# The token's mean as a ninth router column, its variance from ScalarE's squares, and the output bias added in DRAM

## The chip, the cores and the metric

The kernel runs on one core of one Trainium2 chip. The metric is the device time of one execution in microseconds (us), taken as the median of repeated executions. The profile is one further execution, recorded by the hardware profiler; it gives every instruction with its engine, start and duration. The engines are TensorE (PE in the profile; PEld is its weight load), VectorE (DVE, `V` in the code), ScalarE (ACT, `S`), GpSimd (POOL, `G`) and the sync engine (SP, `nc.sync`), which only issues DMAs. L1105 means line 1105 of the kernel.

## What is computed

A hybrid of deformable convolution, attention over the images of the batch and a mixture of experts, on `x` of 4 images, 256 channels, 64 x 64 positions, all in float32:

```python
x = x + conv(group_norm(x), w_off, b_off, w_conv)   # deformable 3x3, 256 -> 256
t = tokens(x)                                       # (4, 4096, 256)
mn = layernorm(t) * gamma + beta
q, k, v = mn @ Wq, mn @ Wk, mn @ Wv                 # 8 heads of 32
g = sigmoid(mn @ Wg + bg)
att = softmax(einsum('slhc,tlhc->sth', q, k) * scale, axis=1)   # s, t: the 4 images
t = t + (einsum('sth,tlhc->slhc', att, v) * g) @ Wo + bo
u = layernorm(t)                                    # no gain, no bias
logits = u @ router_w.T                             # 8 experts, the best 2 of each token
t = t + u + sum over the 2 experts of weight * (gelu(u @ w1 + b1) @ w2 + b2)
x = images(t)
```

A token is one position of one image: there are 16,384, and each has two rows (one for each of its experts).

## The kernel before

It runs in stages, one after the other, with the stages' edges overlapping a little.

**Preparation**, to some 99 us of the span: group norm's statistics, and tables of the images for the gathers.

**A, the deformable convolution** (99 to 2131 us). For each 128 positions and each of 9 taps, POOL gathers four neighbours of 256 channels by an indirect DMA (L577), ACT and DVE weigh and sum them (L593, L601), PE transposes the result (L615), ACT copies it to SBUF (L621) and PE multiplies it by the tap's weights (L640). The weight has 264 columns (`CR = C + NE`, L33): 256 channels, and 8 more that hold the product of the weight with the router's matrix. So a token comes out with its part of the router's logits beside it. The router's columns of a weight are made by `routed` (L133); the image's own part is a small matmul at L634. The sum with the image goes to DRAM as `t1[b][j]`, rows of 264 floats, for image b and block j of 512 positions.

**B, layernorm, q and k** (2131 to 2443 us). For each of 8 blocks and 4 images the loop at L801 loads `t1` (L805), normalizes it (`layernorm`, L176, whose variance goes to POOL's power by `rstd_of`, L162), transposes it into `mn`, projects q and k, and sums their products for the attention's logits (L825).

**D, attention output and routing** (2443 to 2884 us), one call of `block(j)` (L1116) for each of the 8 blocks, with all four images. Its steps, by name:

- `value` projects v of one image and half of the channels (PE); for image 0 ACT writes the first term of the mix. `mixed` adds a further image's term (DVE, 4 instructions of 128x512, L942).
- `gate` is a projection with a sigmoid (PE, ACT L947); `gated` multiplies by it (DVE).
- `output` multiplies by `wo_sb`, again 264 columns wide (L974). `residual` loads `t1` and adds the output bias `bo_sb`, also 264 wide (SP L958, DVE L959). `added` sums the two: the tokens in L988, their router logits in L990; in the first four blocks the tokens go to DRAM too (L994).
- `stats` takes the token's mean and variance by `bn_stats` and `bn_aggr` (DVE, L1001 and L1003, 4 of each an image) and has POOL raise the variance to the power -1/2 (L173). `shift` is minus mean times that (DVE, L1014), and `normed` writes the normalized rows into the tile `u` (ACT, L1021 for the column with the token's number, L1026 for the 256 values).
- `pick` finds the two experts of each token from the logits of all four images (DVE, L1039 to L1057), `count` sums by matmul how many tokens go to each (PE, L1070), and `placed` gives every row its slot (DVE, to L1096).
- `scatter(most)` issues up to that many of the 32 row scatters of a block: an indirect DMA of POOL (L1105) that writes 128 rows of `u` to their slots in `xs_rows`.

The routing of block j is finished inside block j+1: image 3's `shift` and `normed`, then `pick`, `count`, `placed` and all its scatters stand among the steps of the next block. The order of the instructions of PE, DVE and ACT is the one in which `block` writes them. POOL's and SP's is the scheduler's, except that `in_turn` (L153) keeps every power behind the scatters issued before it, and every scatter behind the last power. So a `stats` written behind `scatter(4)` has its power behind those four.

**The experts** (2884 to 3507 us): 142 tiles of 256 rows, each fetched from `xs_rows`, multiplied by its expert's two weights and scattered to `ys_rows`. The last block's routing is done among the first tiles, by a schedule `at(n, ...)` of steps between tile n and the next (L1454 to L1475). SP's and POOL's order is written out here as well (L1477). **The tail**, to 3577 us, adds the results up and stores them.

Of the kernel before, what the change touches and what calls it, by code (L numbers as in the profile page):

```python
# [9 lines left out]
F32 = mybir.dt.float32  # L10
# [22 lines left out]
CR = C + NE  # L33
# [37 lines left out]
def conv_attn_moe_kernel(  # L71
# [32 lines left out]
    nhalf = const.tile([P, 4], F32, name="nhalf")  # L104
# [27 lines left out]

    def routed(rows, rw, ps_turned, ps_out, pool, name):  # L133


        pr = ps_out.tile([P, len(rows), NE], F32, name=f"{name}_pr", tag="om")
        for n, w in enumerate(rows):
            tp = ps_turned.tile([P, C], F32, name=f"{name}_tp{n}", tag="tp")
            for ch in range(NCH):
                T.transpose(tp[:, ch * P : (ch + 1) * P], w[:, ch * P : (ch + 1) * P], ident)  # L140
            wT = pool.tile([P, C], F32, name=f"{name}_wT{n}", tag="sT")
            S.copy(wT, tp)
            for ch in range(NCH):
                T.matmul(
                    pr[:, n, :], wT[:, ch * P : (ch + 1) * P], rw[:, ch, :],
                    start=(ch == 0), stop=(ch == NCH - 1),
                )
        for n, w in enumerate(rows):
            V.tensor_copy(w[:, C:], pr[:, n, :])

    issued = []

    def in_turn(ins, others):  # L153

        for other in others:
            tc.add_manual_dep(
                ins.ins, other.ins.name,
                mybir.DependencyInfo(mybir.DependencyClass.NoSync, mybir.DependencyReason.DATA),
                reason="order of issue",
            )  # L160

    def rstd_of(pool, var, n, name, twice=False, into=None):  # L162


        ve = pool.tile([P, n], F32, name=f"{name}_ve", tag=f"ve{n}")
        if twice:
            V.tensor_scalar(ve, var, 1.0 + EPS, EPS * EPS, ALU.mult, ALU.add)  # L167
        else:
            V.tensor_scalar(ve, var, EPS, None, ALU.add)
        r = into  # L170
        if into is None:
            r = pool.tile([P, n], F32, name=f"{name}_rstd", tag=f"rstd{n}")
        issued.append(G.tensor_tensor(r, ve, nhalf[:, :n], ALU.pow))  # L173
        return r
# [24 lines left out]
    with ExitStack() as actx:  # L199
# [51 lines left out]
        rwc_sb = load_weight(aw, router_w, "rwc_sb")  # L251
# [507 lines left out]
    rw_sb = load_weight(dw, router_w, "rw_sb")  # L759
# [12 lines left out]
    with ExitStack() as bctx:  # L772
# [9 lines left out]
        with ExitStack() as ectx:  # L782
            et = ectx.enter_context(tc.tile_pool(name="e_t", bufs=1))
            ps_e = ectx.enter_context(tc.tile_pool(name="ps_e", bufs=1, space=PSUM))
            routed([wo_sb[:, ch, :] for ch in range(NCH)], rw_sb, ps_tp, ps_e, et, "wo")

            alike = et.tile([P, NCH, P], F32, name="alike")
            V.tensor_copy(alike, bo_c.unsqueeze(2).to_broadcast([P, NCH, P]))
            pb = ps_e.tile([P, 2, NE], F32, name="pb", tag="om")
            for n in range(2):  # L790
                for ch in range(NCH):
                    T.matmul(
                        pb[:, n, :], alike[:, ch, :] if n == 0 else ones, rw_sb[:, ch, :],
                        start=(ch == 0), stop=(ch == NCH - 1),
                    )
            V.tensor_copy(bo_sb[:, C:], pb[:, 0, :])
            V.tensor_copy(rsum, pb[:, 1, :])
        head_sum = block_diagonal(bw, "head_sum", DHEAD, 1.0)
        parts = bw.tile([P, NCH, B * B, NBLK], F32, name="parts")

        for j in range(NBLK):  # L801
            qs, ks = [], []
            for b in range(B):
                rows = bt.tile([P, NT, CR], F32, name=f"bt{b}_{j}", tag="t")
                nc.sync.dma_start(rows, t1[b][j])  # L805
                t = rows[:, :, :C]
                layernorm(bs, t, t, f"l1_{b}_{j}", twice=True)
                mn = channel_major(b, j)
# [21 lines left out]


# [84 lines left out]
    with ExitStack() as bctx:  # L916
# [36 lines left out]
        def residual(j, b):  # L953
            for i in range(0, NT, 2):
                t = ts[j, b, i] = bt.tile(
                    [P, 2, CR], F32, name=f"dt{b}_{j}_{i}", tag="t", bufs=4
                )
                nc.sync.dma_start(t, t1[b][j][:, i : i + 2])  # L958
                V.tensor_tensor(t, t, bo_sb.unsqueeze(1).to_broadcast([P, 2, CR]), ALU.add)  # L959
# [19 lines left out]
        def added(j, b):  # L979
            r = token_major(b, j)  # L980
            if b == 0:
                ss[j] = bs.tile([P, NG, NE], F32, name=f"s{j}", tag="s")
# [13 lines left out]
        def stats(j, b):  # L996
            x_ = token_major(b, j)
            st = bs.tile([P, NT, V.BN_STATS_DIM], F32, name=f"l3st{b}_{j}", tag="ln_st")
            mv = bs.tile([P, NT, V.BN_AGGR_DIM], F32, name=f"l3mv{b}_{j}", tag="ln_mv")
            for i in range(NT):  # L1000
                V.bn_stats(st[:, i, :], x_[:, i, :])  # L1001
            for i in range(NT):
                V.bn_aggr(mv[:, i, :], st[:, i, :])  # L1003
            rstd_of(
                bs, mv[:, :, 1], NT, f"l3_{b}_{j}", into=lns[j][0][:, b * NT : (b + 1) * NT]
            )
            in_turn(issued[-1], scattered)
            scattered.clear()
            lns[j, b] = mv

        def shift(j, b):
            r, nb = (x[:, b * NT : (b + 1) * NT] for x in lns[j])
            mv = lns.pop((j, b))
            V.scalar_tensor_tensor(nb, mv[:, :, 0], -1.0, r, ALU.mult, ALU.mult)  # L1014

        def normed(j, b):
            x_ = token_major(b, j)
            r, nb = lns[j]
# [4 lines left out]
            )  # L1023
            for i in range(NT):
# [8 lines left out]
        def pick(j):  # L1033


            r, nb = lns.pop(j)
            lg = ss.pop(j)
# [78 lines left out]
        def block(j):  # L1116
# [6 lines left out]
            value(j, 1, 1)  # L1123
            residual(j, 0)
            if last:
                shift(j - 1, 3)
                normed(j - 1, 3)
# [4 lines left out]
            mixed(j, 1, 0)  # L1132
            if last:
                count(j - 1)
            value(j, 2, 1)
            mixed(j, 1, 1)
            if last:
                placed(j - 1)
            scatter(14)
            value(j, 3, 0)  # L1140
            mixed(j, 2, 0)
            residual(j, 1)
            value(j, 3, 1)
            mixed(j, 2, 1)
# [11 lines left out]
            stats(j, 0)  # L1156
# [4 lines left out]
            shift(j, 0)  # L1161
            normed(j, 0)
            stats(j, 1)
            scatter(4)
            output(j, 2)
            residual(j, 2)
            gated(j, 3)
            output(j, 3)
            shift(j, 1)
            normed(j, 1)  # L1170
            added(j, 2)
            stats(j, 2)
            scatter(5)
            residual(j, 3)
            shift(j, 2)
            normed(j, 2)
            added(j, 3)
            stats(j, 3)
# [279 lines left out]
    def at(n, fn):  # L1458
        between.setdefault(n, []).append(fn)

    at(0, lambda: (shift(last, 3), normed(last, 3)))
    at(2, lambda: pick(last))
    at(3, lambda: count(last))
    at(4, lambda: placed(last))
    for n in range(6):
        at(6 + n, lambda: next(planning, None))
# [10 lines left out]
    with tc.manual_schedule(engines={nc.sync.engine, nc.gpsimd.engine}):  # L1477
        total = len(tiles)
# [76 lines left out]
```

## Time and profile before

| what | us |
|---|---|
| median of 14 runs | 3573.38 |
| lowest and highest of them | 3560.31, 3600.81 |
| the profiled execution | 3579.29 |
| its span, first to last instruction | 3577.5 |

| busy in the span | us | share | instructions |
|---|---|---|---|
| PE | 3052.5 | 85% | 13658 |
| DVE | 2600.9 | 73% | 6747 |
| POOL | 1973.3 | 55% | 1801 |
| ACT | 1719.8 | 48% | 3913 |

The groups that the change touches:

| instructions | count | busy us | mean ns |
|---|---|---|---|
| PE L640, 128x264 | 4608 | 1323.1 | 412 |
| PE L974, 128x264 | 512 | 118.0 | 386 |
| POOL L1105, row scatters | 256 | 261.4 | 1021 |
| DVE L942, mixes | 192 | 129.7 | 741 |
| POOL L173 in B, powers 128x4 | 32 | 34.4 | 1076 |

A busy share is an average over stages with different limits. It says which engine has how much to do, not what the end waits for. For that one needs the stage by itself (windows of time), and in it the order of the instructions of an engine with the idle time before each and what ended it.

### The profile page before, as it was taken

The numbers are of one execution on the slowest core, as the hardware profiler recorded it, in microseconds if no ns is written. First come the engines' busy times: TensorE is split into PE (matmuls) and PEld (weight loads), VectorE is DVE, ScalarE is ACT, GpSimd is POOL, SyncE is SP. The second block draws the span as 40 slices with busy tenths as digits, with TensorE's granted clock in tenths as the row PEclk, the third lists the DMA queues.
The fourth block names the chain that finished last, engine by engine and source line by source line (L and its number), as shares of the span: only waits on it lengthen the run. The fifth ranks groups of instructions, "written<-read, shape, count | busy, mean of one in ns | idle before, by whom it ended". The sixth has DMA issues, their size and how long they took to land. (4 is left out here: it accounts for less than half of the span.)

```text
span 3577.5 us, 49706 instructions
## 1 busy us (share of the span) xinstructions
PE 3052.5 (85%) x13658; PEld 2232.1 (62%) x13658; DVE 2600.9 (73%) x6747; ACT 1719.8 (48%) x3913; POOL 1973.3 (55%) x1801
## 2 busy tenths in 40 slices
PE   6799997889987899978778779897888888999995
PEld 4567766667766576756656654443444467888883
DVE  3777786867776777876767668887888864557777
ACT  2456654556554555644434434443333344556562
POOL 1665666666677665676776651110666656554441
PEclk7899998999998999988989989999999989999995
DMA  7889998899988899988778861112544344537778
GB/s 233 320 315 331 351 340 332 305 355 353 356 330 338 299 349 330 371 304 295 281 293 315 304 231 61 61 49 85 174 160 143 108 127 130 161 124 246 240 245 305
DMA packets 322442, 898.89 MB, mean 251 GB/s; under 512 B 43218, under 2 KB 89949, under 8 KB 320120
## 3 DMA queue, kind: packets, MB, share of 16 engines
q0 software_dynamic: 191808, 671.74, 51.7%
q1 hardware_dynamic: 130360, 223.98, 19.4%
q8 instruction: 113, 1.85, 0.2%
q14 instruction: 161, 1.32, 0.1%
HBM read 744.43 MB, written 154.79 MB: 251 GB/s over the span
## 5 line engine op out<-in xcount | busy, mean ns | idle before, releaser
L601 DVE SCALAR_TENSOR_TENSOR s<-g,wts,s 128x256 f32<-128x256 f32 x3456 | 1431.7, 478 | 522.5 <-ACT s L593 354.0
L577 POOL DMA_INDIRECT g<-table,idx x1152 | 1339.0, 1162 | 710.1 <-DVE s L601 426.9
L640 PE MATMUL acc<-wconv_sb,sT 128*128 128x264 f32 x4608 | 1323.1, 412 | 271.6 <-ACT sT L621 144.2
L640 PEld LDWEIGHTS acc<-wconv_sb,sT 128*128 128x128 f32 x4608 | 828.0, 200 | 412.7 <-ACT sT L621 170.7
L621 ACT COPY sT<-tps 128x256 f32<-128x256 f32 x1152 | 425.9, 370 | 756.2 <-PE tps L615 499.0
L593 ACT ACTIVATE s<-g,wts 128x256 f32<-128x256 f32 x1152 | 588.9, 511 | 213.5 <-DMA g<-table,idx 191.6
L615 PE MATMUL tps<-ident,s 128*128 128x128 f32 x2304 | 461.0, 283 | 38.6 <-DVE s L601 35.0
L615 PEld LDWEIGHTS tps<-ident,s 128*128 128x128 f32 x2304 | 326.2, 148 | 263.3 <-issue 174.1
L1379 POOL DMA_INDIRECT ys_rows<-y,to x284 | 283.5, 998 | 292.3 <-DVE y L1376 225.1
L1105 POOL DMA_INDIRECT xs_rows<-u,slots x256 | 261.4, 1021 | 128.4 <-issue 113.5
L1350 PE MATMUL ph<-xT,w 128*128 128x256 f32 x1136 | 280.0, 390 | 24.8 <-DVE second L1336 10.7
L1368 PE MATMUL py<-w,hT 128*128 128x256 f32 x1136 | 270.8, 382 | 0.0
L1373 DVE TENSOR_TENSOR y<-py,w 128x512 f32<-128x512 f32 x142 | 98.1, 691 | 204.3 <-ACT w L1312 71.1
L1354 ACT ACTIVATE hT<-ph,w 128x256 f32<-128x256 f32 x284 | 133.6, 474 | 233.4 <-PE ph L1350 177.0
L1350 PEld LDWEIGHTS ph<-xT,w 128*128 128x128 f32 x1136 | 209.8, 195 | 52.9 <-ACT hT L1354 11.6
L1368 PEld LDWEIGHTS py<-w,hT 128*128 128x128 f32 x1136 | 218.2, 192 | 30.5
L173 POOL TENSOR_TENSOR l_rstd<-l_ve,nhalf 128x4 f32<-128x4 f32 x32 | 34.4, 1076 | 252.5 <-DVE l_ve L167 252.5
L825 DVE SCALAR_TENSOR_TENSOR junk<-q,k 128x512 f32<-128x512 f32 x256 | 160.9, 681 | 9.9 <-ACT k L818 9.9
L396 PE MATMUL po<-xs,woff_sb 128*96 128x512 f32 x324 | 167.1, 601 | 0.0
L947 ACT ACTIVATE gate<-pg,bg_c 128x512 f32<-128x512 f32 x64 | 43.9, 686 | 248.0 <-PE pg L748 184.6
L942 DVE SCALAR_TENSOR_TENSOR mix<-pv,att,mix 128x512 f32<-128x512 f32 x192 | 129.7, 741 | 3.1 <-PE pv L748 3.1
L974 PE MATMUL po<-wo_sb,mix 128*128 128x264 f32 x512 | 118.0, 386 | 0.0
(245 smaller groups left out, 3363.5 us busy)
## 6 DMA issues: line engine op xcount, KB each, us to landing
xt<-xs_rows SPq DMA_DIRECT2D x142, 260.0 KB
table<-zt SPq DMA_DIRECT2D x128, 256.0 KB
early_state<-ys_rows SPq DMA_DIRECT2D x128, 256.0 KB
g<-table,idx POOLq DMA_INDIRECT x1152
t<-o SPq DMA_DIRECT2D x32, 528.0 KB
bt<-t SPq DMA_DIRECT2D x32, 528.0 KB
dt<-t SPq DMA_DIRECT2D x64, 264.0 KB
xraw<-in_x SPq DMA_DIRECT2D x16, 1024.0 KB
```

Of the source, the lines that this page charges most:

```text
L396: T.matmul(t["po"], woff_sb[:, ch, ki].rearrange("p kj o -> p (kj o)"), t["xs"][:, ch, ki : ki + RB], start=(n == 0), stop=(n == NCH * 3 - 1),
L577: g = G.indirect_dma_start(out=gs[n % NGB], out_offset=None, in_=tables[b], in_offset=bass.IndirectOffsetOnAxis(ap=params[b][0][:, r, k : ...
L593: first = S.activation(ss[n], gs[n % NGB][:, :C], AF.Copy, scale=params[b][1][:, 0, r, k : k + 1])
L601: last_corner[n] = V.scalar_tensor_tensor(ss[n], gs[n % NGB][:, c * C : (c + 1) * C], params[b][1][:, c, r, k : k + 1], ss[n], ALU.mult, A ...
L615: T.transpose(tps[n][:, ch * P : (ch + 1) * P], s[:, ch * P : (ch + 1) * P], ident)
L621: S.copy(sTs[n], tps.pop(n))
L640: T.matmul(accs[n // K2][:, :CR], sT[:, ch * P : (ch + 1) * P], wconv_sb[:, ch, k, :], start=False, stop=(k == K2 - 1 and ch == NCH - 1),)
L825: V.scalar_tensor_tensor(junk, qs[s_][:, ch, :], 1.0, ks[t_][:, ch, :], ALU.mult, ALU.mult, accum_out=parts[:, ch, s_ * B + t_, j : j + 1],)
L1105: s = G.indirect_dma_start(out=rows_, out_offset=bass.IndirectOffsetOnAxis(ap=slots[:, k, n : n + 1], axis=0), in_=u[:, n % NT, :], in_off ...
L1350: T.matmul(ph, w1_sb[:, ch, f * P : (f + 1) * P], xT[:, ch, :], start=(ch == 0), stop=(ch == NCH - 1),)
L1368: T.matmul(py[:, i, :], hT[:, f, i * P : (i + 1) * P], w2_sb[:, f, :], start=(f == 0), stop=(f == NCH - 1),)
L1379: s = G.indirect_dma_start(out=ys_rows[g], out_offset=bass.IndirectOffsetOnAxis(ap=to[:, i : i + 1], axis=0), in_=y[:, i, :], in_offset=No ...
```

## The change

**A ninth router column.** `NX = NE + 1` and `CR = C + NX` = 265. `load_router` fills the new column of the router's matrix with -1/256, so that a product with it is minus the mean of the 256 channels. Through `routed` the column goes into the convolution's weight, `wo_sb` and `bo_sb`; `t1` has rows of 265 floats; `ss[j]` holds eight logits and minus the mean of each token.

**The variance by ACT.** `stats` is gone, with its `bn_stats`, `bn_aggr` and power for each image. `squares` has ACT square each token's values with minus the mean as bias and sum them as it goes; the squares themselves are written to `u`, which `normed` overwrites later. `rstd(j, half)` takes the variances of two images at once: one DVE instruction and one power of 128x8. `shift` covers two images too.

**The output bias.** `residual` no longer adds `bo_sb`. In B, `with_bias` has POOL issue a DMA for each block and image that adds `bo_sb` to `t1` in DRAM, behind the layernorm of the next one. B's load takes 256 of a row's 265 floats.

**The order.** The power of images 2 and 3 moves to the next block, ahead of `mixed(j, 1, 0)`, and `shift` ahead of `mixed(j, 1, 1)`; `normed` of these images stands between later values. `mixed(j, 2, 0)` and `mixed(j, 2, 1)` stand ahead of `placed`. The power of images 0 and 1 stands behind `added(j, 2)`. The last block's routing begins at the same tile and its placement comes a tile later. In the expert stage `in_turn` does nothing.

```diff
-CR = C + NE
+NX = NE + 1
+CR = C + NX
...
+    def load_router(pool, name):
+        t = pool.tile([P, NCH, NX], F32, name=name)
+        G.memset(t[:, :, NE:], -1.0 / C)
+        nc.sync.dma_start(t[:, :, :NE], router_w.rearrange("(ch p) o -> p ch o", p=P))
+        return t
...
+        def with_bias(b, j):
+            G.dma_start(
+                t1[b][j], bo_sb.unsqueeze(1).to_broadcast([P, NT, CR]), accum_op=ALU.add
+            )
...
-                rows = bt.tile([P, NT, CR], F32, name=f"bt{b}_{j}", tag="t")
-                nc.sync.dma_start(rows, t1[b][j])
-                t = rows[:, :, :C]
+                t = bt.tile([P, NT, C], F32, name=f"bt{b}_{j}", tag="t")
+                nc.sync.dma_start(t, t1[b][j][:, :, :C])
                 layernorm(bs, t, t, f"l1_{b}_{j}", twice=True)
+                if loaded:
+                    with_bias(*loaded.pop())
+                loaded.append((b, j))
...
                 nc.sync.dma_start(t, t1[b][j][:, i : i + 2])
-                V.tensor_tensor(t, t, bo_sb.unsqueeze(1).to_broadcast([P, 2, CR]), ALU.add)
...
-        def stats(j, b):
-            x_ = token_major(b, j)
...
+        def squares(j, b):
+            x_, mean = token_major(b, j), ss[j][:, :, NE:]
+            u = us[j, b] = bu.tile([P, NT, ROW], F32, name=f"u{b}_{j}", tag="u")
+            S.activation(
+                u[:, :, C:], place, AF.Copy, bias=float((b * HB + j % HB) * BLK)
+            )
+            if b % 2 == 0:
+                lns[j, b // 2] = bs.tile([P, 2 * NT], F32, name=f"l3var{b}_{j}", tag="var")
             for i in range(NT):
+                n = b * NT + i
+                S.activation(
+                    u[:, i, :C], x_[:, i, :], AF.Square, bias=mean[:, n],
+                    accum_out=lns[j, b // 2][:, n % (2 * NT)].unsqueeze(1),
+                )
...
+        def rstd(j, half):
+            var = lns.pop((j, half))
+            V.tensor_scalar(var, var, 1.0 / C, EPS, ALU.mult, ALU.add)
+            issued.append(
+                G.tensor_tensor(lns[j][0][:, pair(half)], var, nhalf, ALU.pow)
             )
             in_turn(issued[-1], scattered)
             scattered.clear()
...
+        def shift(j, half):
+            r, nb = (x[:, pair(half)] for x in lns[j])
+            V.tensor_tensor(nb, ss[j][:, pair(half), NE], r, ALU.mult)
```

The order in `block(j)` after the change; `last` steps are left out in the first block:

```python
value(j, 0, 0); value(j, 0, 1); value(j, 1, 0)
residual(j, 0)
rstd(j - 1, 1)                       # last
mixed(j, 1, 0)
value(j, 1, 1)
shift(j - 1, 1)                      # last
mixed(j, 1, 1)
gate(j, 0)
pick(j - 1)                          # last
value(j, 2, 0)
mixed(j, 2, 0)
normed(j - 1, 2); count(j - 1)       # last
value(j, 2, 1)
mixed(j, 2, 1)
normed(j - 1, 3); placed(j - 1)      # last
scatter(14)
residual(j, 1)
...
added(j, 0)
scatter(4)
gated(j, 2); gate(j, 3); added(j, 1)
squares(j, 0)
output(j, 2); residual(j, 2); gated(j, 3)
squares(j, 1)
output(j, 3)
scatter(4)
added(j, 2)
rstd(j, 0)
scatter(5)
residual(j, 3)
squares(j, 2)
added(j, 3)
shift(j, 0)
squares(j, 3)
normed(j, 0); normed(j, 1)
scatter(len(waiting))
```

```diff
-    at(0, lambda: (shift(last, 3), normed(last, 3)))
-    at(2, lambda: pick(last))
-    at(3, lambda: count(last))
-    at(4, lambda: placed(last))
+    at(0, lambda: rstd(last, 1))
+    at(1, lambda: (shift(last, 1), normed(last, 2)))
+    at(2, lambda: (pick(last), normed(last, 3)))
+    at(4, lambda: count(last))
+    at(5, lambda: placed(last))
     for n in range(6):
-        at(6 + n, lambda: next(planning, None))
+        at(7 + n, lambda: next(planning, None))
...
+        fixed.append(True)
```

## The prediction

> **What bounds the kernel now.** The profiled execution took 3579.29 us with a span of 3577.5 us; the median of the 14 runs, 3573.38, is 5.9 us under it. Differences are worked out against the profiled execution and then set on the median. I first cut the span into stages with the view by windows. The offset convolution and small edges aside, three stages carry the change: the convolution A to 2131, layernorm and q/k (B) to 2443, attention output and routing (D) to 2884; the expert stage follows.
>
> ```profile
> core 0: us, PE busy (x) PEld busy (x) DVE busy (x) ACT busy (x) POOL busy (x), PEclk, DMA share, GB/s
> 99.00:2131.00 2032.00, 1723.81 (x8461) 1323.47 (x8461) 1491.66 (x3687) 1060.04 (x2674) 1334.22 (x1162) 0.94 0.89 323
> 2131.00:2443.00 312.00, 269.99 (x786) 132.63 (x786) 259.13 (x935) 120.38 (x195) 34.96 (x35) 0.93 0.17 55
> 2660.00:2715.00 55.00, 47.33 (x135) 25.04 (x134) 48.07 (x134) 18.76 (x42) 38.28 (x37) 0.94 0.37 122
> ```
>
> A is held by its DMA engines (share 0.89) and PE (85% busy). B is held by PE and DVE. The last line is one block of D: PE and DVE each have about 7 us to spare, POOL 17. So none is full, and the question is what the block waits for. The timeline of POOL and then of DVE over one block answers it.
>
> ```profile
> 2617.00 0.95 POOL L1105 DMA_INDIRECT xs_rows<-u,slots  x1 [6.27 <-issue]
> 2618.26 0.96 POOL L1105 DMA_INDIRECT xs_rows<-u,slots  x1 [0.30 <-issue]
> ...
> 2637.44 1.35 POOL L173 TENSOR_TENSOR rstd<-l_ve,nhalf 128x4 f32<-128x4 f32 x1 [1.30 <-DVE l_ve L169]
> ...
> 2657.43 0.96 POOL L1105 DMA_INDIRECT xs_rows<-u,slots  x1 [0.30 <-issue]
> 2658.42 1.04 POOL L173 TENSOR_TENSOR rstd<-l_ve,nhalf 128x4 f32<-128x4 f32 x1
> 2659.66 1.04 POOL L1105 DMA_INDIRECT xs_rows<-u,slots  x1 [0.20 <-DVE shift L1014]
> ...
> 2664.84 0.96 POOL L1105 DMA_INDIRECT xs_rows<-u,slots  x1 [0.30 <-issue]
> 2672.08 0.95 POOL L1105 DMA_INDIRECT xs_rows<-u,slots  x1 [6.28 <-issue]
> ```
>
> ```profile
> 2659.49 0.16 DVE L1014 SCALAR_TENSOR_TENSOR shift<-l3mv,rstd 128x4 f32<-128x4 f32 x1 [3.19 <-POOL rstd L173]
> 2664.85 5.33 DVE L942 SCALAR_TENSOR_TENSOR mix<-pv,att,mix 128x512 f32<-128x512 f32 x8
> 2671.86 0.17 DVE L1096 CAST slots<-row 128x16 int32<-128x16 f32 x1
> ```
>
> The columns are start, duration, instruction, and in brackets the idle time before it. POOL issues 32 row scatters a block, 0.96 us each and 0.30 to the next. Its fourth rstd power stands behind 27 of them; DVE waits 3.19 us for it (shift, L1014); then DVE's pick, eight mixes and placement run to the slots at 2671.86, and the next block's first scatter starts at 2672.08. POOL does 5 left-over scatters meanwhile and then idles. This is a loop: scatters, power, DVE chain, scatters. First scatters lie at 2508.04, 2564.07, 2617.00, 2672.08, 2733.02, 2789.29 and 2842.58, a mean of 334.54 / 6 = 55.76 us. From power's start to first scatter it is 12.5 to 12.6 us in most blocks.
>
> **Stage D after the change.** The built order has POOL do 22 scatters, the power of images 0 and 1, the other 10 scatters, and then the power of images 2 and 3. All 32 scatters now lie ahead of the power that frees the next placement.
> - POOL: from 2617.00 to 2658.42 are 41.42 us, less the 1.30 of idle 40.1; another block gives 39.3; I take 39.7 for 27 scatters and 3 powers. Five more scatters, 5 × 1.27 = 6.35. Two powers fewer at 1.4 (mean 1.34 by the groups, and a gap), −2.8. Width: 128x2 costs 726 ns (L330), 128x4 1007 ns (L173 in B), 0.14 us a column, so 128x8 is 0.56 longer; the value lies between nothing (fixed cost only) and double (1.3). Sum 39.7 + 6.35 − 2.8 + 0.56 = 43.8 to the second power's start, and its own 1.6.
> - Chain: before, power (1.04), shift, pick, 8 mixes, placement = 12.58, of which the chain less the power is 11.5. After, four more mixes stand behind shift: mixed(j,1,1) ahead of pick, mixed(j,2,0) and (j,2,1) ahead of placement, so 12 × 0.666 instead of 8 (5.33 / 8): 11.5 + 2.7 = 14.2. count's matmuls wait behind the value matmuls, as before.
> - Period 43.8 + 1.6 + 14.2 = 59.6, and late scatters (1.5 to 1.67 us in some) 0.9: I take 60.5, bounds 58.7 and 61. Six periods × 4.7 = +28.
>
> What the change removes in D, per block: DVE's 16 bn_stats (5.6 us), 16 bn_aggr (1.4), the four epsilon adds, three shifts and 8 bias adds (8 × 0.66 = 5.3), some 12.3 us. DVE spends it waiting: it stands at shift until POOL comes. ACT gains 16 squares at 0.52 (the 4 of L1026 take 2.07), 8.3 us on 18.8 of 55; that is hidden, since the first pair's variance is ready 25 to 26 us after the placement and POOL reaches its power after 22 × 1.27 = 28. Were that cover gone, each us later would cost one. What is late next is the gates and the output of the block, 27.4 us after the first scatter (36.2 before); they wait on DVE and PE, which have room.
>
> Edges. The first stream starts 16 us after block 0's last addition now; then 26.6: squares 2.6, the power 1.6, two images normed on ACT 4.1 ahead of block 1's first values 2.4, mixes, pick 5.2, mixes 5.4, placement 1.9 and waits. With DVE's gains in block 0 that is 2517.1 for 2508.04: +9.1. At the end the last addition comes 36.2 us after the last first scatter now and 27.4 then, −8.7. The expert stage starts with four squares' and one norm's work more on ACT, its count two tiles later: +1, between −2 and +5 (one tile is 623 / 142 = 4.4).
>
> **A.** 4608 matmuls of 264 columns become 265: 386 ns at 264, 379 at 256, 592 at 512, so 0.83 to 0.88 ns a column, 3.8 us of PE. Bounds: nothing (DMA share 0.89), and 8 columns' price at once, 6.7 ns × 4608 = 31, of which PE's share of the chain would pass on a third, 10. I take +1. The wider t1 rows (1060 B for 1056) are nothing measurable.
>
> **B.** 32 bias additions are issued by POOL behind each layernorm's power. No row shows an accumulating DMA. Its issue costs POOL at least 0.3 (a DMA issue on SP's queue, 0.32), at most four scatters, 5.1. I take 1.27. POOL is busy 35 of 312 us; powers come 4.4 to 6 us apart in bursts of four and then pause 21 us. At 1.27 a power is never late; at 5.1 three powers a block of B come 1.7 late: 8 × 3 × 1.7 = 41, the upper bound; DVE and PE stand behind them. The loads on SP have 512 runs of 1 KB instead of 128 of 4224 B: the first loads make DVE wait 6.23, 2.99 and 2.29 now, so 0 to +5; I take 0. Three buffers let them be fetched ahead.
>
> The Trainium skill, "DMA: Bandwidth & Descriptors", section "Anatomy of one DMA — SWDGE (gpsimd) path", puts some 2 us on such a DMA, most of it completion, and lets many descriptors go out before an increment shows; by it the upper 41 would be 0. No run here shows it yet.
>
> **Sum.** +28 + 9.1 − 8.7 + 1 + 1 = +30: span 3607.9, median 3573.4 + 30 = 3603.
>
> Two rules of the Trainium skill bear on the move of the squares, one each way. "Perfetto Trace Analysis", section "Optimizing Scalar/DVE Operations", says that where DVE is saturated some of its work may go to ScalarE; by it the first rival below would be the answer, −35. The row against it is the 3.19 us that DVE waits for POOL in a block where it is busy for 48 of 55. "ScalarE: Activation LUTs", section "Rules for kernel authors", wants multiplies on VectorE; here the 16 cost 8.3 us for 5.6, by it 2.7 us a block (+16 in six) were ACT what the block waits for, and its 19 of 55 busy say it isn't.
>
> **Rivals.**
> 1. Faster: the block follows its engines. Freed of 12.3 us, DVE would have 36, PE's 47.3 would set the pace, with 2.6 of waits some 50 a block: 6 × −5.8 = −35, so 3540. For it: PE and DVE are the busiest in the window. Against it: POOL's loop, which PE doesn't enter. It decides if 32 scatters, two powers and the chain of 14.2 fit in 50: a scatter slot under 1.0 (now 1.27), or the second power ahead of the last ten. 10%.
> 2. No change: POOL's loop as shortened by two powers, with scatters that run back to back at 1.2 and pick's chain overlapped by DVE's new idle time, gives 54.5 to 56: 3565 to 3575. For it: POOL idles 1.30 at the first power now. Against: mixed(1,1), 2.7 us, is behind shift in DVE's written order. 8%.
> 3. Slower through B: the bias additions delay the powers, at up to +41 beside D's +30, 3625 to 3645. For it: no price in the trace. Against: POOL is idle for nine tenths of B. 5%.
> 4. The change doesn't do what it says, for instance through ACT's table loads between Square and Sigmoid: the built orders hold 7 loads each, so 1%.
>
> **How the numbers follow.** The forecast, D's longer loop, has 76%, with its own range 3590 to 3615: period bounds 58.7 to 61 give +18 to +32 (six periods), edges and A and B −5 to +10. Runs scatter by 20 us about their median, which adds a few us to the median. For 8 in 10 the range reaches to 3575 below, which leaves the faster rival out, and to 3622 above. A difference of 0.3%, 10.7 us, is about what a measurement of this kernel tells from none. Faster: rival 1 and a little of 2, 0.12; same: rival 2 and the forecast's lowest end, 0.08; slower: the forecast and rival 3, 0.80.
>
> **What would show it.** Right: POOL's first scatters some 60 us apart; both powers 128x8 at about 1.6, the second right behind the 32nd scatter; DVE waiting over 15 us a block at shift; from power to first scatter 15 to 16 us. B and A within 5 us of before. Wrong: first scatters 50 us apart and POOL idle ahead of the second power (rival 1); the 128x8 power at 3 us or more; B's powers each late behind a bias DMA (rival 3); the sum of A's matmuls up by more than 10 us.

## The result and the profile after

The changed kernel takes 3667.27 us (median of 10 runs, 3651.7 to 3692.25) against 3577.91 for the kernel before (47 runs, 3550.45 to 3600.81): a ratio on record of 1.0257, 95% interval 1.0231 to 1.0283 (the two medians alone give 1.025). It is slower, as forecast, but by 89 us and not by 30, and outside the range. The profiled execution has a span of 3690.4 us, 113 more than that of before; it took 3692.11 us, 25 above the median, so the profile shows more than the median tells.

The windows of the changed kernel, by the same stages and for one block of D (columns as before: the stretch, its length, then each engine's busy time with the number of instructions, PE's granted clock, the DMA engines' share, GB/s):

```profile
99.00:2143.00 2044.00, 1740.68 (x8455) 1330.04 (x8455) 1492.39 (x3687) 1057.83 (x2673) 1308.32 (x1163) 0.93 0.89 321
2143.00:2461.00 318.00, 271.62 (x791) 133.03 (x790) 260.48 (x934) 120.67 (x196) 74.00 (x65) 0.93 0.60 110
2608.00:2675.00 67.00, 50.20 (x137) 28.41 (x136) 34.11 (x77) 27.25 (x74) 35.17 (x34) 0.85 0.44 148
```

DVE has lost 14 us of work in a block (48.07 to 34.11; 12.3 forecast) and ACT gained 8.5 (18.76 to 27.25; 8.3 forecast); PE's 50 us now lie in 67 us and not in 55. Where the 113 us of the profile went, by the ends of the stages and POOL's first scatters:

| stretch | before | after | difference | forecast |
|---|---|---|---|---|
| start to the end of A | 2128.7 | 2143.6 | +15 | +1 |
| B | 313.3 | 317.3 | +4 | 0 |
| B's end to the first scatter | 66.1 | 77.3 | +11 | +9.1 |
| six periods of first scatters | 334.5 | 409.2 | +75 | +28 |
| last first scatter to the first expert tile | 42.9 | 46.6 | +4 | −8 |
| experts and tail | 692.0 | 696.4 | +4 | 0 |

The period of a block rose from 55.76 to 68.2 us, and not to 60.5. POOL's timeline shows in which part of the loop:

```profile
2608.20 1.04 POOL L1133 DMA_INDIRECT xs_rows<-u,slots  x1 [17.71 <-issue]
...
2635.79 0.96 POOL L1133 DMA_INDIRECT xs_rows<-u,slots  x1 [0.30 <-issue]
2641.46 1.67 POOL L1039 TENSOR_TENSOR rstd<-l3var,nhalf 128x8 f32<-128x8 f32 x1 [4.71 <-DVE l3var L1037]
...
2655.76 1.67 POOL L1039 TENSOR_TENSOR rstd<-l3var,nhalf 128x8 f32<-128x8 f32 x1
2675.32 1.04 POOL L1133 DMA_INDIRECT xs_rows<-u,slots  x1 [17.88 <-issue]
```

The 22 scatters end 28.6 us after the first, where they were expected; but then POOL stands 4.7 us for the variance. (In the six other blocks it is 5.7 to 8.5.) The second power follows behind the other ten scatters, and the next block's first scatter 19.6 after the start of that power instead of 15.8. So the variance was late. The timelines of PE, ACT and DVE in the same block say why:

```profile
2622.72 3.59 PE L756 MATMUL pg<-early_state,wg_sb 128*128 128x512 f32 x8
2626.15 3.74 PE L992 MATMUL po<-wo_sb,mix 128*128 128x265 f32 x16
2640.70 6.42 PE L992 MATMUL po<-wo_sb,mix 128*128 128x265 f32 x16 [10.81 <-DVE s L1008]
```

```profile
2619.34 0.69 ACT L966 ACTIVATE gate<-pg,bg_c 128x512 f32<-128x512 f32 x1 [1.03 <-PE pg L756]
2630.47 0.69 ACT L966 ACTIVATE gate<-pg,bg_c 128x512 f32<-128x512 f32 x1 [10.45 <-PE po L992]
2635.46 0.69 ACT L966 ACTIVATE gate<-pg,bg_c 128x512 f32<-128x512 f32 x1 [4.30 <-remote]
```

PE's eight matmuls for the gate of image 3 are done by 2626.3, in two halves of four. ACT, idle since 2620.0, has nothing else left to wait for: the updates of PE's semaphore that let its two sigmoids go stand in the trace at 2630.45 and 2635.43, and they start at 2630.47 and 2635.46, 6 and 9 us behind their matmuls. In the block of the kernel before that the prediction shows, each sigmoid of image 3 starts with the end of its matmuls:

```profile
2640.44 3.60 PE L748 MATMUL pg<-early_state,wg_sb 128*128 128x512 f32 x8
2642.36 0.69 ACT L947 ACTIVATE gate<-pg,bg_c 128x512 f32<-128x512 f32 x1 [4.59 <-DVE l3st L1001]
2644.07 0.69 ACT L947 ACTIVATE gate<-pg,bg_c 128x512 f32<-128x512 f32 x1 [1.03 <-PE pg L748]
```

In the changed kernel DVE's addition for image 2, whose matmuls end at 2628.1 and 2629.9, starts at 2639.77, and PE waits 10.81 us for that addition, as its two product buffers are full:

```profile
2639.77 0.69 DVE L1006 TENSOR_TENSOR early_state<-po,dt 128x512 f32<-128x512 f32 x1 [2.91 <-remote]
```

The releaser "remote", in ACT's last line too, says that the trace finds no instruction that ended just before: the semaphore with which PE tells of its results was raised long after the matmuls that raise it.

Below, lateness is measured at the readers of PE's results, the sigmoids of the gate (L966, L947 before) and the additions of the output (L1006, L988 before): how long one starts after both the end of its last matmul and the end of its engine's own earlier work. (The ends of matmuls in a trace are modelled; four matmuls belong to a sigmoid and eight to an addition. The expectations below speak of late completions of PE for the same thing, seen at its semaphore.) In the kernel before no reader in D is more than 1.0 us late. In the changed kernel the latest is 5.9 to 12.9 us late in each of the seven blocks that issue scatters; in block 0, which has none to issue, none is late. The first late reader of a block, an addition of image 1, reads matmuls that ended 12.9 to 14.1 us after the first scatter, some ten scatters into the run; the last late update comes some 3.3 us after the end of the 22nd.

PE was not busy meanwhile, by the windows of 4 us over the same stretch:

```profile
2628.00:2632.00 4.00, 1.89 (x9) 1.27 (x7) 0.69 (x1) 0.69 (x1) 2.88 (x4) 1.00 0.71 239
2632.00:2636.00 4.00, 0.00 (x0) 0.00 (x0) 0.00 (x0) 0.54 (x1) 3.09 (x4) 0.54 0.27 100
2636.00:2640.00 4.00, 0.00 (x0) 0.00 (x0) 0.92 (x2) 4.00 (x18) 0.75 (x1) 0.50 0.19 69
```

Its granted clock falls to 0.5 from 2632.3 on, 2.4 us after its last matmul. The Trainium skill, "TensorE: Matmul & The Clock Gate", section "Part 1: The HAM clock gate (the "warmup" mystery)", says that the gate follows PE's activity and closes after an idle window of about 3.4 us. Here the clock fell sooner than that; the row agrees with the page only in that the clock falls while PE is idle, and so speaks for an idle array whose results were announced late. Nor was it a queue of the scatters' data: counted every 2 us, never more than about two of the scatters issued in this block had packets still to come. What remained was POOL's new order, with 22 scatters on end where there were 14, 4, 4, 5, 5 with powers between.

### The profile page after: what moved, and what is told of

It reads as the page before. It is cut to its first block, busy times and chain, and to the rows that moved or that the text cites. A ratio compares the mean times of both kernels' runs of the same rounds, so it can differ in the third digit from the quotient of the medians.

```text
span 3690.4 us, 49706 instructions
## 1 busy us (share of the span) xinstructions
PE 3089.1 (84%) x13658; PEld 2255.0 (61%) x13658; DVE 2512.3 (68%) x6395; ACT 1781.3 (48%) x4169; POOL 1959.9 (53%) x1819
## 4 chain that ended last, share of the span: by engine, by line
PE 46%; issue 15%; POOL 11%; DVE 10%; DMA 8%; another core or an unknown queue 5%; ACT 4%; SPq 0%; DVEq 0%; POOLq 0%; ACTq 0%
PE acc L648 12%; POOL g L585 10%; DMA g<-table,idx 6%; PE ph L1379 6%; PE py L1397 5%; PE po L404 4%; DVE s L609 3%; PE tps L623 3%; PE pq L756 3%; PE pk L756 3%; PE po L992 2%; PE pg L756 2%; PE pv L756 2%; PE tpx L1358 1%
## 5 line engine op out<-in xcount | busy, mean ns | idle before, releaser
L585 POOL DMA_INDIRECT g<-table,idx x1152 | 1312.7, 1139 | 750.8 <-DVE s L609 473.2
L648 PE MATMUL acc<-wconv_sb,sT 128*128 128x265 f32 x4608 | 1340.8, 416 | 277.3 <-ACT sT L629 177.1
L1133 POOL DMA_INDIRECT xs_rows<-u,slots x256 | 250.7, 979 | 202.6 <-issue 201.1
L1379 PE MATMUL ph<-xT,w 128*128 128x256 f32 x1136 | 278.3, 388 | 29.3 <-DVE second L1365 19.6
L1379 PEld LDWEIGHTS ph<-xT,w 128*128 128x128 f32 x1136 | 207.5, 193 | 58.3 <-ACT w L1341 16.3
L992 PE MATMUL po<-wo_sb,mix 128*128 128x265 f32 x512 | 136.8, 423 | 82.1 <-DVE s L1008 75.8
L992 PEld LDWEIGHTS po<-wo_sb,mix 128*128 128x128 f32 x512 | 106.8, 211 | 118.1 <-issue 54.6
L966 ACT ACTIVATE gate<-pg,bg_c 128x512 f32<-128x512 f32 x64 | 44.0, 687 | 276.9 <-PE pg L756 136.0
```

Of the source, the lines that this page charges most:

```text
L585: g = G.indirect_dma_start(out=gs[n % NGB], out_offset=None, in_=tables[b], in_offset=bass.IndirectOffsetOnAxis(ap=params[b][0][:, r, k : ...
L648: T.matmul(accs[n // K2][:, :CR], sT[:, ch * P : (ch + 1) * P], wconv_sb[:, ch, k, :], start=False, stop=(k == K2 - 1 and ch == NCH - 1),)
L992: T.matmul(po[:, n, :CR], o[:, ch, (i + n) * P : (i + n + 1) * P], wo_sb[:, ch, :], start=(ch == 0), stop=(ch == NCH - 1),)
L1379: T.matmul(ph, w1_sb[:, ch, f * P : (f + 1) * P], xT[:, ch, :], start=(ch == 0), stop=(ch == NCH - 1),)
```

## The experiments

Each ratio is to the kernel before on the same chip; the chips' own medians of before lay between 3531 and 3578 us. Theory 1 is that a long unbroken run of row scatters on POOL holds up PE's completions; theory 2 that the odd width of 265 does; the third candidate is the forecast's loop alone.

**The column alone.** The kernel before with `CR = C + NX`, `load_router` and `ss` of nine columns, B's load as in the change; nothing reads the mean.

> The kernel before with the ninth router column alone (product rows of 265 floats; the layernorm stage loads 256 of them, since the tiles would not fit otherwise); nothing reads the mean, and order, statistics and bias stay. In the changed kernel PE's completions in stage D come up to 10 us later than the records of its matmuls say, once a block, and two blocks' first scatters stand 68.2 us apart. Theory 1 (a long unbroken run of row scatters on POOL holds PE's completions up): no such delay here, first scatters 55 to 57 us apart, time within 0 to +8 us of before. Theory 2 (the odd width of 265 slows PE): the delay is here too, first scatters 62 us apart or more, +35 us or more. The convolution stage: 0 to +10 by the forecast, +15 by the one profile of the changed kernel.

Ratio 0.9989 (0.9959 to 1.0019). First scatters 54.9 us apart, no reader in D over 0.1 us late; A ended at 2075.6 us in a profile of 3518.6. Theory 2 falls, and the column costs nothing that can be measured, in A either. A's +15 above was not the column's: A ended between 2122.3 and 2136.1 in two further profiles with it (the breaks below) and at 2127.8 in one without, all on a chip where before took 3575.

**The bias alone.** The kernel before with `with_bias` in B and without DVE's addition of the bias in `residual`.

> The kernel before with the output bias alone moved: POOL's 32 adding DMAs in the layernorm stage, loads of 256 of a row's 264 floats there, and no addition of the bias by DVE in stage D (5.3 us a block less of DVE's work). By the forecast DVE's time in stage D is not what a block waits for: first scatters stay within 1 us of 55.8 us apart, and the layernorm stage grows by 0 to 5 us; time from -3 to +8 us. The rival (DVE's relief reaches the end): the period falls by up to 5 us, -30 us.

Ratio 1.0029 (0.9999 to 1.0059), first scatters 55.7 us apart (55.76 before): 5.3 us of DVE's work a block taken away changed a block by nothing. That is no clean answer to the rival, though: with the split of before, 14, 4, 4, 5, 5, readers come 2.6 to 4.6 us late here in each of the seven blocks, and POOL waits 3.5 us a block for the variances of its powers (1.5 before), so a part of the relief may be hidden. B grew from 313.3 to 315.9 us. The DMA's issue costs POOL 1.24 us (median of the 32 in the changed kernel, 1.27 taken).

**A longer run in the kernel before.** Same work, same order of the other engines:

```diff
-            scatter(14)
+            scatter(22)
...
-            scatter(4)
+            scatter(2)
...
-            scatter(4)
+            scatter(2)
...
-            scatter(5)
+            scatter(1)
```

> The kernel before with its 32 scatters split 22, 2, 2, 1, 5 in place of 14, 4, 4, 5, 5 around the same four powers: 27 still lie ahead of the last power, and the work is the same. Theory 1: PE's completions now come late in stage D, 5 to 10 us at the third and fourth image of a block, and the time rises by 20 us or more. Theory 2, or a cause in the new order of the other engines: no late completions, and the time stays within 10 us of before (the first powers come later, which DVE and ACT have room for).

Ratio 1.0133 (1.0075 to 1.0192), first scatters 61.3 us apart, the latest reader of a block 3.9 to 9.8 us late. Its timeline of ACT shows the same stall (scatters from 2583.00):

```profile
2601.28 0.69 ACT L947 ACTIVATE gate<-pg,bg_c 128x512 f32<-128x512 f32 x1 [1.03 <-issue]
2616.33 0.69 ACT L947 ACTIVATE gate<-pg,bg_c 128x512 f32<-128x512 f32 x1 [14.35 <-PE po L974]
```

The matmuls of that gate were done by 2608.2. Theory 1 holds without any part of the change: a split of scatters alone costs 5.5 us a block (6.4 against the 54.9 of the column alone, which ran on the same chip). Its first power comes later too, some 29 us after the first scatter for some 20 before, and what that alone costs is not parted from it.

**A pause in the changed kernel.** Three idle powers of 128x8 behind the first 11 of the 22.

```diff
-            scatter(14)
+            scatter(11)
+            if last:
+                pause(3)
+            scatter(3)
```

> The changed kernel with three idle powers of 128x8 on POOL (5 us of work that nobody reads) behind the first 11 of the 22 scatters. Theory 1: with the run of scatters broken PE's completions come on time again (gates of image 3 within 1 us of their matmuls, no wait of ACT there), and the 5 us that POOL loses are taken from its wait of 5 to 8 us for the variance: the time stays within 10 us of 3667 though POOL has 5 us a block more to do. The plain loop without theory 1: the delay stays and each block is 5 us longer, +30 or more, 3697.

Ratio 1.0206 (1.0145 to 1.0267), first scatters 66.5 us apart, no sigmoid over 0.3 and no addition over 1.9 us late. POOL did 5 us more a block and the block was no longer than in the changed kernel (68.2, and 66.3 in a second profile of it). The variance of images 0 and 1 is ready 22.3 to 22.7 us after a block's first scatter, and POOL reaches its first power without a wait in all seven blocks. In the block whose first scatter is at 2540.54:

```profile
2563.10 0.17 DVE L1037 TENSOR_SCALAR l3var<-l3var 128x8 f32<-128x8 f32 x1 [0.51 <-ACT u L1026]
2573.74 1.67 POOL L1039 TENSOR_TENSOR rstd<-l3var,nhalf 128x8 f32<-128x8 f32 x1
```

So one pause of 5.1 us in 22 scatters gives the readers back their time. What remains is the loop with the pause in it: 61.4 us a block without its 5.1.

**Breaks of two lengths.** After every 4th of a block's first 20 scatters `rest()`: a memset of 128x2 (0.11 us), or a power of 128x2 (0.73 us).

```diff
         def scatter(most):
             for _ in range(min(most, len(waiting))):
+                if not fixed and 10 < len(waiting) < 32 and len(waiting) % 4 == 0:
+                    rest()
```

> The changed kernel with a tiny POOL instruction that nobody needs (a memset of 128x2) after every 4th of the block's first 20 scatters. If any instruction of POOL's own between the scatters lets PE's completions through, they come on time again and first scatters stand 60 to 62 us apart, as the forecast had it, in place of 68.2: some 45 us less than the changed kernel, a ratio of about 1.013 to before. If it takes a pause of some length, nothing changes: 68 us, ratio 1.025.

> The same with a power of 128x2 (0.73 us) in the memset's place, five a block, so that POOL pauses its scatters about as long and as often as the kernel before does with its powers. POOL has 5.4 us a block more to do. If such a pause lets PE's completions through: no late completions, the first power some 5 us later than its variance, first scatters 65 to 66 us apart (the loop of the forecast, 60.5, with 5.4 more ahead of the second power). If the unbroken length does not matter and only POOL's share of time does: late completions stay, and the period is 68 to 73 us.

With the memset: ratio 1.0251 (1.0205 to 1.0297), 66.5 us a block, the latest reader of a block 4.4 to 15.0 us late. The time is no better than the changed kernel's (median 3668.6, and 3645.8 with the power, on one chip), but the memset is not without effect: in three of the seven blocks the sigmoids are on time, POOL reaches its first power without a wait, and only the additions of images 2 and 3 are late (5.4 to 6.4 us); these blocks take 63.5 to 64.6 us. With the power: ratio 1.0184 (1.0126 to 1.0242), 65.8 us, no sigmoid late and no addition over 2.5 us. POOL and ACT in a block of the latter, whose first scatter is at 2643.75:

```profile
2648.01 0.96 POOL L1143 DMA_INDIRECT xs_rows<-u,slots  x1 [0.30 <-issue]
2648.99 0.73 POOL L1135 TENSOR_TENSOR idle<-idle_in,nhalf 128x2 f32<-128x2 f32 x1
2649.91 1.04 POOL L1143 DMA_INDIRECT xs_rows<-u,slots  x1 [0.19 <-issue]
...
2675.42 0.96 POOL L1143 DMA_INDIRECT xs_rows<-u,slots  x1 [0.30 <-issue]
2676.40 1.67 POOL L1039 TENSOR_TENSOR rstd<-l3var,nhalf 128x8 f32<-128x8 f32 x1
```

```profile
2659.33 0.69 ACT L966 ACTIVATE gate<-pg,bg_c 128x512 f32<-128x512 f32 x1 [4.61 <-PE pg L756]
2661.05 0.69 ACT L966 ACTIVATE gate<-pg,bg_c 128x512 f32<-128x512 f32 x1 [1.03 <-PE pg L756]
```

The gates of image 3 start with the end of their matmuls, and POOL reaches its first power without a wait. The variance is ready 22.3 to 22.8 us after the first scatter, as with the pause. 0.73 us of other work every fourth scatter is enough; 0.11 is not. Whether a break acts by its length or by the slower mean pace that it brings (22 scatters in 32 to 33 us with the power or the pause, in 28 without) these runs don't tell. What is left is the loop: five idle powers (3.7 us) less, an estimated 62.1 us a block.

**The second power earlier.** `rstd(j, 1)` moved from the next block to a place behind `squares(j, 3)`, ahead of the last ten scatters, and `scatter(5)` behind the first power left out.

> The changed kernel with one move: the power of images 2 and 3 stands behind the power of images 0 and 1, ahead of the last ten scatters of the block, so that 22 scatters lie ahead of it and not 32. If the loop of the forecast (scatters, power, chain to the placement) is what holds a block: the power starts some 41 us after the block's first scatter and the next first scatter follows 19 to 20 us later, 61 us a block instead of 68.2, and the time falls by some 45 us to about 3625; by theory 1 PE's late completions stay, as the 22 scatters are still unbroken. If the loop is not what holds it (the late completions of PE alone do, or the engines' work), the time stays within 10 us of the changed kernel's 3667.

Ratio 1.0183 (1.0128 to 1.0238), 64.9 us a block, the latest reader of a block 6.2 to 7.8 us late. The power came 39.9 us after the first scatter, as expected, but the next first scatter 25.1 after it, not 19 to 20: ACT normed images 0 and 1 (4.0 us) ahead of copying the next block's first values, PE waited 3.1 us for a buffer that those copies free, and DVE's mixes for both. The loop was cut, and the next wait took half or more of the gain: 3.3 us a block against the changed kernel's 68.2, 1.4 against the 66.3 of its second profile, 7 expected. The ratio is no lower than in the changed kernel's second measurement below.

**The changed kernel again**, beside the two that follow.

> The changed kernel once more beside these, on the same chip: ratio 1.023 to 1.028 to before, first scatters 67 to 69 us apart, PE's completions up to 10 us late once a block.

Ratio 1.0185 (1.0119 to 1.0251), 66.3 us a block, the latest reader of a block 5.7 to 7.9 us late. It lies below the range expected for it: the same kernel differs by 0.7% between two chips, so differences of that size between kernels of different chips are not read here.

**The order redone.** All parts of the change kept:

```python
mixed(j, 1, 0); value(j, 1, 1)
shift(j - 1, 1); normed(j - 1, 0)
gate(j, 0)
normed(j - 1, 1); pick(j - 1); normed(j - 1, 2); count(j - 1)
mixed(j, 1, 1); value(j, 2, 0)
normed(j - 1, 3); placed(j - 1)
scatter(14)
mixed(j, 2, 0); value(j, 2, 1); mixed(j, 2, 1)
...
added(j, 2); rstd(j, 0)
scatter(8)
squares(j, 2); added(j, 3); shift(j, 0); squares(j, 3)
rstd(j, 1)
scatter(len(waiting))
```

with an idle power of 128x2 behind the 5th, 10th, 18th and 27th scatter; and the same without the idle powers.

> The changed kernel with its parts kept and its order redone by what the runs showed: the second power ahead of the last ten scatters; the power of images 0 and 1 behind the 14th scatter; four idle powers of 128x2 that break the scatters into runs of 4 or 5; images 0 and 1 normed behind the next block's first values; shift and pick ahead of mixed(j,1,1), which then covers count; mixed(j,2,*) behind the placement. Without late completions the last addition comes some 31 us after the first scatter (26.2 in the run with idle powers, and 5.4 of mixes more), and the next first scatter 18 us later: 49 to 52 us a block, PE (47 busy) and POOL (48) both near full. Against before 6 x -4 to -6, -25 to -35 us, ratio 0.991 to 0.994. If the loop is not the bound, the period stays at 56 or more.

> The same order without the four idle powers. POOL has 3.8 us a block less to do, but its scatters run 10 and 14 on end with hardly a pause between them. By theory 1 PE's completions come late again and the block is 3 to 8 us longer than with the idle powers; without theory 1 it is equal or up to 2 us shorter.

With idle powers: ratio 0.9975 (0.9942 to 1.0009), 55.9 us a block. In five of the seven blocks the latest reader is still 4.0 to 6.3 us late. They are just those at whose start the last five scatters of the block before and the first five of this one stand on end, ten without a break; ahead of the other two there is no scatter, or a gap of 1.2 us, and none of their readers is late. The five take no longer for it, though (54.5 to 55.7 us where a period is measured, 57.8 in the other two). Without: 1.0165 (1.0104 to 1.0226), 64.1 us, the latest reader 5.0 to 16.3 us late in six of the seven blocks; the one without a late reader takes 55.7 us, those with one 58.0 to 71.5. The worst, in the block whose first scatter is at 2509.85:

```profile
2512.47 1.98 PE L756 MATMUL pg<-early_state,wg_sb 128*128 128x512 f32 x4 [0.83 <-issue]
2531.52 3.78 PE L756 MATMUL pg<-early_state,wg_sb 128*128 128x512 f32 x4 [17.07 <-ACT gate L966]
```

```profile
2530.78 0.69 ACT L966 ACTIVATE gate<-pg,bg_c 128x512 f32<-128x512 f32 x1 [19.48 <-remote]
```

Four matmuls end at 2514.45, their sigmoid starts 16.3 us later, 3.5 after the end of the run of scatters (24 on end, the last at 2526.4), and PE waits 17.07 us for it. Taking 3 us of useless work off POOL made a block 8 us longer on average, which is theory 1 at its plainest. The period of 49 to 52 was missed: POOL stood 7.2 to 11 us at its first power, placed too early behind 14 scatters; that kept scatters 9 to 16 from landing in time, and ACT's squares of image 3 waited up to 6.6 us a block for the tile that they free.

**The two powers together.** The same, split 20, 2, 10, with the idle powers behind the 5th, 10th, 15th and 27th.

> The reordered kernel with the scatters split 20, 2, 10 around the two powers in place of 14, 8, 10, and the idle powers behind the 5th, 10th, 15th and 27th. In the reordered kernel the first power stood 7.6 us on POOL for its variance behind 14 scatters, and so scatters 9 to 16 landed late, for which ACT's squares of image 3 waited 6.5 us (their tile). With 20 scatters ahead of the first power that wait goes: the second power starts some 33 us after the block's first scatter and not 39, and the chain of 15.4 follows: 49 to 52 us a block in place of 55.9, ratio to before 0.987 to 0.993. If another wait takes its place (PE's work, 47 us, or late completions), the period stays above 54 and the ratio at 0.997.

Ratio 0.996 (0.9932 to 0.9987), 52.1 us a block. One block has readers up to 5.6 us late, the others at most 2.6. The period is just above the 49 to 52 expected, the ratio above the 0.987 to 0.993 expected; POOL's timeline now has the powers close to each other:

```profile
2636.59 1.67 POOL L1039 TENSOR_TENSOR rstd<-l3var,nhalf 128x8 f32<-128x8 f32 x1 [2.88 <-DVE l3var L1037]
2638.46 1.04 POOL L1143 DMA_INDIRECT xs_rows<-u,slots  x1 [0.20 <-issue]
2639.80 0.96 POOL L1143 DMA_INDIRECT xs_rows<-u,slots  x1 [0.30 <-issue]
2640.82 1.67 POOL L1039 TENSOR_TENSOR rstd<-l3var,nhalf 128x8 f32<-128x8 f32 x1
```

This block begins at 2604.53 and the next at 2656.57; PE is busy 46.6 us of it. From B's end to the first expert tile it takes 416.5 us in this profile against 443.6 before, 27 less; the time shows 0.4%, 11 us by the medians. B is 5.7 us longer in the profile (319.0), experts and tail 4.2; the rest lies within what runs scatter. It is faster than the changed kernel by far and than the kernel before by 0.4%, less than the order of stage D promised.

## Why the prediction was wrong

- **What bounds the kernel before**, the loop of scatters, power, chain and placement, was read rightly as far as the runs show: the bias alone took 5.3 us a block from DVE and left the period at 55.7 (with late readers, so not shown cleanly), and in the last run the loop's parts, moved, changed the period as the loop says.
- **The step that failed** is the cover in stage D: "that is hidden, since the first pair's variance is ready 25 to 26 us after the placement and POOL reaches its power after 22 × 1.27 = 28." POOL did reach it then. The variance came 33 to 37 us after the first scatter, since readers of PE's results were held up to 12.9 us while POOL issued 22 scatters without a break; with the pause or the idle powers between them it came at 22.3 to 22.8, before even the forecast's 25 to 26. The text put a price on the loss of this cover ("each us later would cost one") and did not see what would take it. The term put at nothing is 35.25 us (mean of six blocks, first scatter to first power) less the 28.6 that the run with breaks gives without its five idle powers (32.24 − 3.65): 6.7 a block, 40 us in six.
- **The chain** was mis-sized: 14.2 behind the second power was forecast, 17 measured (18.65 from the power's start, less 1.67), and 17.5 in the run with breaks. One part is a misreading: from the start of the last power, 2658.42, to the first scatter, 2672.08, the lines shown give 13.66 us and not the 12.58 said; 12.6 is the chain without the power, which was then taken off once more. That is 1.1 a block, and the sum should have read 60.7 and 61.6 for its 59.6 and 60.5. The other is a wait: "count's matmuls wait behind the value matmuls, as before" does not hold: `mixed(j,2,1)` waits for `value(j,2,1)`, which PE does behind `count`, 1.8 us of DVE's idle time in the block shown, and the mix behind shift waits 0.74 us for `value(j,1,1)`. +3 a block in all, 18 us. POOL's part was a little shorter than the sum's 43.8 + 1.6, without stragglers. So the loop without late completions is an estimated 62.1 (61.4 by the run with the pause), with 60.5 forecast and 61.6 by the right reading.
- **The edges**: the first stream +11 for +9.1. The end −8.7 was forecast and +4 measured; block 7 has the late completions too.
- **A** +1 was right: the column alone changes nothing. **B** 0 forecast, +4 measured, +2.6 with the bias alone. POOL's powers there start 0.16 us after their variances, so none was late and the bound of 41 was far off. The Trainium skill's page "DMA: Bandwidth & Descriptors", section "Anatomy of one DMA — SWDGE (gpsimd) path", puts most of a DMA's fixed 2 us at completion and calls the making of its descriptors small; here the issue took 1.24 us of POOL, more than that says, but no power waited for it.
- **The rivals**: the faster one (PE's pace) did not come, and would not have come without late completions either, the loop being some 62; its condition, the second power ahead of the last ten scatters, is part of the last run, whose block took 52.1. The slower one through B fell. None named a delay of PE's signals. The range reached to 3622 because its upper end rested on B's price and the period's own bounds, 58.7 to 61; both bounds took for granted that a matmul's result is known when it is done.
- **The sum**: of the profile's +113 the forecast had 30. The rest is +47 in the six periods (75 for 28), +12 at the end of D, +2 at its start, +3 to +4 each in B and in the experts and tail, and +14 in A, which is scatter between runs; without A's part it is +99, nearer to the median's +89.

What stays open: by what path a run of POOL's DMA issues holds up PE's signals and not DVE's or ACT's (in D of the changed kernel one update of theirs comes over 0.3 us after the last end of an instruction), after how many scatters and at what pace of them it begins (below), and whether the recording of the profile has a part in it; no run here was made to tell these.

## What to carry to other kernels

Where POOL issues many indirect DMAs, look for waits that the trace puts down to "remote" or to an instruction long done, and compare the matmuls' ends with their readers' starts: an order of POOL is not only a matter of what comes ahead of what, but of how long a run is. Powers that look like POOL's burden may be the breaks that keep PE's results flowing; when they are merged, put something of their length back in their place. And work taken from an engine that waits in a loop showed nothing here until the loop's own order was redone.

## What the runs showed of the hardware that was not expected

- Runs of 22 scatters (1.27 us each) made the latest reader of PE's results in a block 3.9 to 12.9 us late; 24 on end with hardly a pause up to 16.3; the 22 with one pause of 5.1 us, or with 0.73 us of POOL's own work after every fourth, at most 2.5. A memset of 0.11 us in its place left 4.4 to 15.0.
- The number of scatters alone does not decide. The kernel before and the bias alone both begin a block with 14 ahead of the first power. Before, they take 18.7 to 19.1 us and no reader is over 1.0 us late; with the bias alone they take 17.4 us in five of seven blocks and 18.6 to 18.7 in the other two, and the latest readers come 4.5 to 4.6 and 2.6 to 3.9 us late. In the reordered kernel with idle powers they come 4.0 to 6.3 us late just where a block begins with ten on end. No run varied the pace by itself.
- A power on POOL of 128x8 took 1.67 us; the 0.14 us a column taken from widths of 2 and 4 gave 1.57.
